# Tiles of 16 channels by 8 states in a selective scan: two tiles share one broadcast of du and one GpSimd product

## The chip, the core and the metric

One core of a Trainium2 chip. The metric is the device time of one execution in microseconds. The engines run side by side and wait for one another by semaphores: TensorE (PE, with its weight loads, PEld), VectorE (DVE), ScalarE (ACT), GpSimd (POOL), and SyncE (SP), which here issues nearly all DMAs in its own program order.

## What is computed

Two layers over a batch of 8 images of 64 x 64 pixels and 96 channels, all in float32. Layer 0 is a two-dimensional selective scan block; layer 1 is an MLP between an FFT upsampling and a low-pass with downsampling. Nearly all time goes to the scan of layer 0, which in the reference is

```
h = exp(dl[..., None] * A) * h + (dl * ul)[..., None] * Bl[:, :, None, :]
y = einsum('bkdn,bkn->bkd', h, Cl)
```

for each of 4096 pixels in four directions k, with 192 channels d and 16 states n. So there are 8 x 4 x 192 x 16 recurrences, each 4096 steps long. Directions 0 and 2 walk the image by rows (forward and back), directions 1 and 3 by columns.

## The kernel before

**Tiles.** A scan tile is 128 partitions by T = 1024 pixels: 16 states by 8 channels. A chunk of 1024 pixels of one direction holds 192 / 8 = 24 tiles (NT); a direction has 4 chunks, an image 16, the run 128 chunks or 3072 tiles. Inside a chunk, tile i has q = i // 8, and of i % 8 the lowest bit is s and the rest is j, so tiles i and i + 2 with even j lie side by side in channels.

**The life of a tile t** (line numbers of the profile):

- `fetch` (L1074): SP issues a DMA that spreads 8 rows of du = delta * u from DRAM over 128 partitions, each row 16 times (512 KB), into `dub` (4 buffers). It is issued 6 tiles ahead.
- `product_b` (L1080): GpSimd multiplies `dub` by `br`, the repeated B, into `bb` (4 buffers), 3 tiles ahead.
- `decay` (L1087, L1095): six TensorE matmuls with the 0/1 matrix `sel_b` spread delta over the states into PSUM (`pd`, 2 buffers), and ScalarE takes `exp` of it in place with the rate `neg_a` per partition. It is issued one tile ahead.
- `scan` (L1102): VectorE runs the recurrence over the 1024 pixels.
- `product_c` (L1108): the result times `cr`, the repeated C, on VectorE, or on GpSimd for every third tile (i % 3 == 2, `by_pool`).
- `hold` (L1122): the last column goes to `carry` for the next chunk; by VectorE, or by ScalarE for the tiles with `by_pool`.
- `sums` (L1141): every second tile, TensorE adds two tiles' products over the states with `sel_r` into `py`; `store` copies `py` and writes it to DRAM.

Every engine takes its instructions in program order. The loop at the end of the kernel writes the order out by hand; for tile i it issues

```
fetch(tiles[i + FETCH])            # FETCH = 6
product_c(tiles[i - 1])            # GpSimd's tiles
product_b(tiles[i + LEAD])         # LEAD = 3
decay(tiles[i + 1]); scan(t); product_c(t); hold(t)
side.advance(...)                  # other work, up to a budget
sums(tiles[i - 3 : i - 1])         # odd i
```

**Side work.** Everything else is cut into generators that the class `Side` advances once per tile within budgets per engine (`CAPS`, us per tile, and KB for DMA): normalisation and convolution of the next image (`front`), the preparation of the next chunk (`prepare`: loads of u, projections, delta, `dp`, the product du = delta * u on GpSimd at L1040, and `br` and `cr`), and for the image before the layer norm and gate (`tail`) and the MLP (`mlp`). `prepare` fills `br` and `cr` by DMAs straight from the SBUF tile `xd` (L1005). `front` keeps the image transposed in `xt` and writes it to DRAM by `lay` once all blocks are there, so that the row directions read contiguous rows. `tail` loads the row directions' sum into `ye` as a whole image, and GpSimd adds it block by block (L687). At the end of the run, `tail` and `mlp` of the last image run with no scan beside them.

Of the kernel before, what the change touches and what calls it, by code (L numbers as in the profile page):

```python
# [8 lines left out]
F32 = mybir.dt.float32  # L9
# [29 lines left out]
class Side:  # L39
# [10 lines left out]
    CAPS = dict(pe=(2.5, 3.2), act=(2.3, 3.0), dve=(1.5, 1.5), pool=(1.4, 2.7), dma=(270, 450))  # L50
# [87 lines left out]
def kernel(ctx: ExitStack, tc: tile.TileContext, a: dict, out: bass.AP):  # L138
# [32 lines left out]
    for p in range(2):  # L171
# [21 lines left out]
    neg_a = cp.tile([128, K, NT], F32, name="neg_a")  # L193
    queue().dma_start(
        neg_a.rearrange("p k g -> p (k g)"),
        a["a_logs"].rearrange("(c n) k f q j -> n c (k f q j)", n=NS),
    )

    sel_r = cp.tile([128, 4, 32], F32, name="sel_r")
    queue().dma_start(  # L200
        sel_r.rearrange("p j m -> p (j m)"), a["sel_r"].rearrange("(c n) j m -> n c (j m)", n=NS)
    )

    sel_b = cp.tile([128, 8, NS, 8], BF16, name="sel_b")
# [68 lines left out]
    def constants_in():  # L273
        nc.gpsimd.memset(xp, 0.0)
        raw["sel"] = tile_([128, 8, 128], "sel_0")
        for hf in range(2):
            nc.sync.dma_start(
                raw["sel"][64 * hf : 64 * hf + 64].rearrange("p j m -> p (j m)"),
                a["sel_b"][0:64, 0:2].rearrange("r q j m -> r (q j m)"),
            )  # L280
        raw["dt_b"] = tile_([C, K, HF], "dt_b")
        nc.sync.dma_start(raw["dt_b"], a["dt_b"])
        names = ("xp_dt", "xp_c", "xp_b")
        raw["xp"] = [tile_([128, K, Q3, R if n == "xp_dt" else NS], n) for n in names]
        ds = raw["ds"] = tile_([128, Q3, K], "ds")
        for hf in range(2):
            for q, r0, r1, f, c0 in pieces:
                rows, src = slice(64 * hf + r0, 64 * hf + r1), slice(c0, c0 + r1 - r0)
                for t, name in zip(raw["xp"], names):
                    nc.sync.dma_start(t[rows, :, q, :], a[name][src, :, f, 0 : t.shape[-1]])  # L290
                nc.sync.dma_start(ds[rows, q, :], a["ds"][src, f, :])
        for name, shape in (("coef", [128, 3, 3]), ("w2", [128, 3, C]), ("b2", [128, C])):
            raw[name] = tile_(shape, name)
            nc.sync.dma_start(raw[name], a[name])

    def constants_of_scans():
        yield {}

        nc.scalar.activation(neg_a, neg_a, AF.Exp)
        nc.vector.tensor_scalar(neg_a, neg_a, -1.0, None, ALU.mult)  # L300
        nc.vector.tensor_copy(sel_b, raw["sel"].rearrange("p j (c n) -> p j n c", n=NS))
# [214 lines left out]
    def front(b):  # L516
# [6 lines left out]
        def begin():  # L523
            yield {}
            pad = v["pad"] = bp.tile([C, W + 2, H + 2], F32, tag="pad", name="pad", bufs=1)
            nc.gpsimd.memset(pad[:, 0, :], 0.0)
            nc.gpsimd.memset(pad[:, W + 1, :], 0.0)
            nc.gpsimd.memset(pad[:, 1 : W + 1, 0:1], 0.0)
            nc.gpsimd.memset(pad[:, 1 : W + 1, H + 1 : H + 2], 0.0)
            v["xt"] = [bp.tile([128, H, w], F32, tag=f"xt{w}", name=f"xt{w}", bufs=1) for w in (W, W // 2)]  # L530
            u_dram[b] = [dr.tile([DI, L], F32, tag=f"u{o}", name=f"u{o}") for o in range(2)]
            z_dram[b] = dr.tile([DI, L], F32, tag="z", name="z")

        def piece(g):
# [3 lines left out]
            t = bp.tile([128, 4, C], F32, tag="x", name="x", bufs=4)  # L538
# [34 lines left out]
        def conv(n, g):  # L573
# [5 lines left out]
            for tap in range(9):  # L579
# [11 lines left out]
            xt = v["xt"][n]  # L591
            nc.scalar.copy(
                xt[:, :, 8 * g : 8 * g + 8].rearrange("p h w -> p w h"), e.rearrange("p (i j) -> p i j", i=8)
            )
            for rows, cs, blk in parts_of(n, g):
# [3 lines left out]
                )  # L599

        def lay(n):

            yield {}
            while not all((b, n, blk) in filtered for blk in range(8)):
                yield {}
            for h0 in range(0, H, 8):
                yield dict(dma=262 if n == 0 else 131)
                h1 = h0 + 8
                if n == 0:
                    src = v["xt"][0][:, h0:h1].rearrange("p h w -> p (h w)")  # L610
                    nc.sync.dma_start(u_dram[b][0][0:128, W * h0 : W * h1], src)
                else:
                    u = u_dram[b][0][128:192].rearrange("c (h w) -> c h w", h=H)
                    for p in range(2):
                        nc.sync.dma_start(u[:, h0:h1, 32 * p : 32 * p + 32], v["xt"][1][64 * p : 64 * p + 64, h0:h1])
            yield {}
            laid.add((b, n))
# [21 lines left out]
        lays = [(4, 0, lambda n=n: lay(n)) for n in range(2)]  # L639
# [4 lines left out]
        if b == 0:  # L644
            return start + convs[:4], convs[4:] + lays + gates + [bp.close(), bp.close()]
        return start, convs + lays + gates + [bp.close()]

    def tail(b, keep, pairs=True):
# [3 lines left out]
        def begin():  # L652
# [4 lines left out]
            v["ye"] = [bp.tile([C, H, W], F32, tag=f"ye{f}", name=f"ye{f}", bufs=1) for f in range(HF)]  # L657
            for h0 in range(0, H, 8):
                for f in range(HF):
                    yield dict(dma=200)  # L660
                    nc.sync.dma_start(
                        v["ye"][f][:, h0 : h0 + 8].rearrange("p h w -> p (h w)"),
                        y_dram[b][0][f * C : f * C + C, W * h0 : W * h0 + 8 * W],
                    )
            yield {}
            yield {}

        def block(g):
# [6 lines left out]
            for t, src in zip(yz, (y_dram[b][1], z_dram[b])):  # L675
                for f in range(HF):
# [3 lines left out]
                    )  # L680
            y, z = [yz[0][:, f] for f in range(HF)], yz[1]
            yield {}
            yield {}
            yield dict(pool=2.6)
            for f in range(HF):
                e = v["ye"][f][:, :, 8 * g : 8 * g + 8].rearrange("p h w -> p w h")
# [96 lines left out]
    def mlp(b, keep):  # L783
# [13 lines left out]
        def up_h(j):  # L797
# [3 lines left out]
            for wh in range(2):  # L801
# [4 lines left out]
                s.append(bp.tile([SIDE, MB], F32, tag="t1s", name="t1s", bufs=5))  # L806
# [9 lines left out]
        def fetch_rows(r0):  # L816
            s = v[r0] = bp.tile([128, 5, C], F32, tag="t1r", name="t1r", bufs=4)
# [14 lines left out]
        def rows_(r5):  # L832
# [12 lines left out]
            xu = bp.tile([C, px], F32, tag="xu", name="xu", bufs=4)  # L845
            nc.scalar.activation(xu, t[:C, :px], AF.Identity, scale=got["rs"], bias=got["nb"])  # L846
            for m in range(3):
                yield dict(pe=0.95, act=0.7)
                if m == 0:
                    sq = bp.tile([128, 3, px], F32, tag="mq", name="mq", bufs=3)  # L850
                t = side.again(n, "ph")
                nc.tensor.matmul(t[:, :px], w1[:, m, :], xu, start=True, stop=True)  # L852
                nc.scalar.activation(sq[:, m, :], t[:, :px], AF.Square, bias=b1[:, m : m + 1])  # L853
            yield dict(pe=0.95)
            t = side.again(n, "p3")
            for j in range(15):
# [3 lines left out]
                    t[:SIDE, C * i : C * i + C], sq[:, m, row], w2q[:, m, :], start=(m == 0), stop=(m == 2)  # L860
# [95 lines left out]
    def prepare(b, k, i0, got):  # L956
# [3 lines left out]
        def begin():  # L960
# [4 lines left out]
            assert k % 2 or all((b, n) in laid for n in range(2))  # L965
# [31 lines left out]
        def broadcasts():  # L997

            xd = v["xd"]
            for name, row in (("br", 48), ("cr", 32)):  # L1000
                t = got[name] = pp.tile([128, T], F32, tag=name, name=name)
                for hf in range(2):
                    yield dict(dma=256)
                    src = xd[64 * hf + row : 64 * hf + row + NS, None, :]
                    nc.sync.dma_start(t[:, MB * hf : MB * hf + MB], src.to_broadcast([NS, 8, MB]))  # L1005
# [47 lines left out]
    for b in range(images):  # L1053
        for k in (1, 0, 2, 3):
            order = range(NCH) if k < 2 else range(NCH - 1, -1, -1)
            for n, c in enumerate(order):
                got = {}
                for i in range(NT):
                    q, n8 = divmod(i, 8)
                    s, j = n8 % 2, n8 // 2  # L1060
                    tiles.append(
                        dict(b=b, k=k, i0=c * T, first=n == 0, i=i, q=q, s=s, j=j, g=8 * q + 4 * s + j, got=got)
                    )
# [6 lines left out]
    def fetch(t):  # L1070
        assert t["got"].get("ready", 0) > t["q"]
        t["dub"] = sp.tile([128, T], F32, tag="dub", name="dub", bufs=4)
        g = t["g"]
        nc.sync.dma_start(  # L1074
            t["dub"], t["got"]["du"][None, 8 * g : 8 * g + 8, :].to_broadcast([NS, 8, T])
        )

    def product_b(t):
        t["bb"] = sp.tile([128, T], F32, tag="bb", name="bb", bufs=4)
        nc.gpsimd.tensor_tensor(t["bb"], t["dub"], t["got"]["br"], ALU.mult)  # L1080

    def decay(t):
        pd = t["pd"] = psd.tile([128, T], F32, tag="pd", name="pd")
        for p in range(3):
            for hf in range(2):
# [3 lines left out]
                    sel_b[rows, 4 * t["s"] + t["j"]].rearrange("p n c -> p (n c)"),  # L1089
# [5 lines left out]
        nc.scalar.activation(pd, pd, AF.Exp, scale=neg_a[:, t["k"], t["g"] : t["g"] + 1])  # L1095

    def scan(t):
# [3 lines left out]
        held = carry[:, t["g"] : t["g"] + 1]  # L1101
# [4 lines left out]
    def product_c(t):  # L1106
        t["hc"] = sp.tile([128, T], F32, tag="hc", name="hc", bufs=4)
        (nc.gpsimd if t["by_pool"] else nc.vector).tensor_tensor(t["hc"], t["h"], t["got"]["cr"], ALU.mult)  # L1108
# [9 lines left out]
    def hold(t):  # L1118
        if t["last"]:
# [3 lines left out]
            carry[:, t["g"] : t["g"] + 1], t["h"][:, end : end + 1]  # L1123
# [8 lines left out]
    def sums(two):  # L1132
# [5 lines left out]
        for t in two:  # L1138
            for hf in range(2):
# [3 lines left out]
                    sel_r[:, t["j"], :],  # L1143
# [40 lines left out]
    LEAD, FETCH = 3, 6  # L1184

    with tc.manual_schedule():
# [8 lines left out]
        side.urgent = prepare(0, tiles[0]["k"], tiles[0]["i0"], tiles[0]["got"])  # L1195
# [4 lines left out]
        for i in range(FETCH):  # L1200
            fetch(tiles[i])
            if i >= FETCH - LEAD:
                product_b(tiles[i - FETCH + LEAD])
# [3 lines left out]
        for i in range(n + 4):  # L1207
# [41 lines left out]
            if i + FETCH < n:  # L1249
                fetch(tiles[i + FETCH])  # L1250
            if 0 < i <= n and tiles[i - 1]["by_pool"]:
                product_c(tiles[i - 1])
            if i + LEAD < n:
                product_b(tiles[i + LEAD])
# [112 lines left out]
```

## Time and profile before

| | |
|---|---|
| time, median of 3 runs | 10879.19 us (10876.58 to 10884.08) |
| the profiled execution | 10889.88 us, its span 10888.1 us |
| granted TensorE clock | 0.977 |
| busy | POOL 93%, DVE 92%, PE 86%, ACT 63% |
| DMA | 2402.30 MB, queue q1 87.0% of 16 engines |
| first product of B on GpSimd, and the last scan | start at 136.8 and 10610.4 us |

A group of instructions is read as: line, engine, operation, tile written <- tiles read, count, then busy time in us and mean ns of one, then the engine's idle time ahead of them with what ended most of it. A line of waits gives the total us, the number of waits and the longest.

### The profile page before, as it was taken

The page shows a single profiled execution, that of the slowest core. Times are in us where ns is not written, and L with a number is a line of the kernel's source. Part 1 is how long each engine was busy: PE and PEld are TensorE (multiplying, and loading weights), DVE is VectorE, ACT ScalarE, POOL GpSimd, SP SyncE. Part 2 cuts the span into 40 slices and gives each one's busy share as a digit, 9 for nine tenths or more (in the row PEclk, how much of TensorE's full clock was granted, in tenths as well). Part 3 has the DMA queues.
Part 4 walks back from the last instruction along what each step waited for, and adds up shares of the span by engine and source line. Part 5 has one row for each costly group of instructions (what it writes and reads, how often), then busy time and mean ns, then how long its engine had stood idle before and what let it go on. Part 6 is the DMA issues. An engine that isn't in the chain of part 4 may idle for free. (4 is left out here: it accounts for less than half of the span.)

```text
span 10888.1 us, 152912 instructions
## 1 busy us (share of the span) xinstructions
PE 9406.6 (86%) x52498; PEld 3129.1 (29%) x52498; DVE 9965.6 (92%) x7319; ACT 6891.4 (63%) x10138; POOL 10172.5 (93%) x4674
## 2 busy tenths in 40 slices
PE   7788778988789988899889997898978989789888
PEld 2222222422233222332223322233222432223325
DVE  5999999999999999999999999999999999999990
ACT  5666556767567665666656666566756767566653
POOL 4999999999999999999999999999999999999990
PEclk8999999999999999999999999999999999999998
DMA  6879898898988989898998989899898898988981
GB/s 155 224 200 234 218 236 216 221 235 232 239 214 225 235 233 233 214 225 232 240 228 220 230 223 247 217 225 234 231 237 218 222 232 234 239 214 223 230 207 49
DMA packets 1052725, 2402.30 MB, mean 221 GB/s; under 512 B 302012, under 2 KB 322748, under 8 KB 1051944
## 3 DMA queue, kind: packets, MB, share of 16 engines
q1 hardware_dynamic: 1050968, 2391.48, 87.0%
q8 instruction: 413, 6.77, 0.3%
q14 instruction: 368, 3.01, 0.1%
q10 hardware_dynamic: 976, 1.04, 0.0%
HBM read 1929.05 MB, written 328.73 MB: 207 GB/s over the span
## 5 line engine op out<-in xcount | busy, mean ns | idle before, releaser
L1080 POOL TENSOR_TENSOR bb<-dub,br 128x1024 f32<-128x1024 f32 x3072 | 7183.5, 2367 | 149.2 <-DMA dub<-du 95.6
L1095 ACT ACTIVATE pd<-pd,neg_a 128x1024 f32<-128x1024 f32 x3072 | 3339.4, 1087 | 3051.3 <-PE pd L1087 3026.1
L1102 DVE TENSOR_TENSOR_SCAN pd<-pd,carry,bb 128x1024 f32<-128x1024 f32 x1536 | 3605.4, 2347 | 279.3 <-ACT pd L1095 162.6
L1087 PE MATMUL pd<-dp,sel_b 64*128 64x512 bf16 x18432 | 2596.7, 385 | 1075.4 <-DVE carry L1122 686.6
L1108 DVE TENSOR_TENSOR hc<-pd,cr 128x1024 f32<-128x1024 f32 x2048 | 2508.7, 1225 | 144.8 <-PE py L1141 3.2
L1108 POOL TENSOR_TENSOR hc<-h,cr 128x1024 f32<-128x1024 f32 x1024 | 2423.0, 2366 | 180.3 <-DVE h L1102 151.4
L1102 DVE TENSOR_TENSOR_SCAN h<-pd,carry,bb 128x1024 f32<-128x1024 f32 x768 | 1797.5, 2341 | 1.7 <-ACT pd L1095 1.6
L1141 PE MATMUL py<-hc,sel_r 128*32 128x512 f32 x12288 | 1736.0, 620 | 48.6 <-POOL hc L1108 47.1
L1087 PEld LDWEIGHTS <-sel_b 64*128 64x128 bf16 x18432 | 722.7, 94 | 3602.7 <-issue 1557.1
L1102 DVE TENSOR_TENSOR_SCAN pd<-pd,bb 128x1024 f32<-128x1024 f32 x512 | 1173.3, 2292 | 128.2 <-ACT carry L1122 52.2
L565 PE MATMUL pc<-pad,convr 96*128 96x512 f32 (+1 forms) x2304 | 844.0, 610 | 2.1 <-issue 2.1
L1115 PE MATMUL idle<-xp,ident 128*128 128x384 f32 x1450 | 662.9, 540 | 3.2 <-ACT t1s L807 3.2
L1102 DVE TENSOR_TENSOR_SCAN h<-pd,bb 128x1024 f32<-128x1024 f32 x256 | 583.7, 2280 | 14.8 <-ACT pd L1095 11.6
L1040 POOL TENSOR_TENSOR u<-dl,u 128x512 f32<-128x512 f32 x384 | 491.7, 1280 | 108.7 <-ACT dl L1035 108.7
L1017 PE MATMUL pv<-xd,dt_w 64*64 64x512 f32 x1536 | 425.4, 632 | 166.9 <-ACT xd L994 164.5
L1141 PEld LDWEIGHTS py<-hc,sel_r 128*32 128x32 f32 x12288 | 253.4, 109 | 977.2 <-issue 751.4
L859 PEld LDWEIGHTS p<-w2q,mq 128*100 128x100 f32 x4800 | 461.9, 168 | 169.3 <-issue 135.2
L852 PE MATMUL ph<-xu,w 96*128 96x500 f32 x960 | 493.6, 617 | 16.0 <-ACT xu L846 9.2
L859 PE MATMUL p<-w2q,mq 128*100 128x96 f32 x4800 | 504.2, 256 | 2.3 <-ACT mq L853 2.3
L1032 PE MATMUL pv<-e,ident 128*128 128x512 f32 x768 | 437.1, 651 | 27.9 <-ACT pv L1030 27.0
L1042 ACT CAST dp<-pv 128x512 bf16<-128x512 f32 x768 | 452.1, 589 | 5.0 <-PE pv L1041 5.0
L984 PE MATMUL px<-u,xp 64*64 64x512 f32 x1536 | 417.2, 618 | 5.1 <-DMA u<-u 3.2
(162 smaller groups left out, 8195.4 us busy)
## 6 DMA issues: line engine op xcount, KB each, us to landing
dub<-du SPq DMA_DIRECT2D x3072, 512.0 KB
u<-u SPq DMA_DIRECT2D x768, 128.0 KB
du<-u SPq DMA_DIRECT2D x768, 128.0 KB
y<-yq SPq DMA_DIRECT2D x768, 128.0 KB
br<-xd SPq DMA_DIRECT2D x256, 256.0 KB
cr<-xd SPq DMA_DIRECT2D x256, 256.0 KB
yp<-y SPq DMA_DIRECT2D x384, 128.0 KB
yp<-u SPq DMA_DIRECT2D x192, 128.0 KB
```

Of the source, the lines that this page charges most:

```text
L565: nc.tensor.matmul(t[rows].rearrange("p (i j) -> p i j", i=8), weights[:, cs], v["pad"][:, 8 * blk + kw : 8 * blk + kw + 8, kh : kh + H], ...
L852: nc.tensor.matmul(t[:, :px], w1[:, m, :], xu, start=True, stop=True)
L859: nc.tensor.matmul(t[:SIDE, C * i : C * i + C], sq[:, m, row], w2q[:, m, :], start=(m == 0), stop=(m == 2))
L1040: nc.gpsimd.tensor_tensor(v["u"][:, q, :], dl, v["u"][:, q, :], ALU.mult)
L1042: nc.scalar.copy(dp[:, p, :], t)
L1080: nc.gpsimd.tensor_tensor(t["bb"], t["dub"], t["got"]["br"], ALU.mult)
L1087: nc.tensor.matmul(pd[:, MB * hf : MB * hf + MB], sel_b[rows, 4 * t["s"] + t["j"]].rearrange("p n c -> p (n c)"), t["got"]["dp", t["q"]][r ...
L1095: nc.scalar.activation(pd, pd, AF.Exp, scale=neg_a[:, t["k"], t["g"] : t["g"] + 1])
L1102: nc.vector.tensor_tensor_scan(t["h"][:, ::step], pd[:, ::step], t["bb"][:, ::step], 0.0 if t["first"] else held, ALU.mult, ALU.add)
L1108: (nc.gpsimd if t["by_pool"] else nc.vector).tensor_tensor(t["hc"], t["h"], t["got"]["cr"], ALU.mult)
L1115: nc.tensor.matmul(p, ident, xp[:, 0:2].rearrange("p k q r -> p (k q r)"), start=True, stop=True)
L1141: nc.tensor.matmul(py[r0 : r0 + 32], sel_r[:, t["j"], :], t["hc"][:, MB * hf : MB * hf + MB], start=(t["j"] == 0), stop=(t["j"] == 3 and t ...
```

## The change

Partitions of a scan tile become 16 channels by 8 states. The tiles i and i + 2 (j even and odd) now hold the same 16 channels with the lower and the upper 8 states (`half`). They share one `dub` (16 rows of du, each 8 times, 512 KB), and one GpSimd instruction over 2 x 1024 elements multiplies it by both halves of `br`. `br` is now 2 x 1024 wide and `cr` has a tile for each half; both are read from a DRAM copy `bc` of the B and C rows, and the second half of `cr` is read at a chunk's last tile. `neg_a`, `sel_b` and `sel_r` are laid out to fit. To make room, the transposed pieces shrink: `xt` holds 16 of the 64 columns and is written out in runs of 16 floats as soon as two blocks are there, `ye` is read in pieces of 16 columns per block pair, and `x`, `t1s`, `t1r`, `xu` and `mq` have fewer buffers. The DMA budget of the side work rises.

```diff
-    CAPS = dict(pe=(2.5, 3.2), act=(2.3, 3.0), dve=(1.5, 1.5), pool=(1.4, 2.7), dma=(270, 450))
+    CAPS = dict(pe=(2.5, 3.2), act=(2.3, 3.0), dve=(1.5, 1.5), pool=(1.4, 2.7), dma=(450, 700))
...
+        def lay(n, two):
+            yield {}
+            xt, u = v[n, two], u_dram[b][0].rearrange("c (h w) -> c h w", h=H)
+            for h0 in range(0, H, 16):
+                yield dict(dma=131)
+                h = slice(h0, h0 + 16)
+                for rows, cs, blk in parts_of(n, 2 * two):
+                    nc.sync.dma_start(u[cs, h, 8 * blk : 8 * blk + 16], xt[rows, h, :])
...
+            if ("ye", g // 2) not in v:
+                ye = v["ye", g // 2] = bp.tile([C, HF, H, 16], F32, tag="ye", name="ye", bufs=2)
+                for f in range(HF):
+                    src = y_dram[b][0][f * C : f * C + C].rearrange("c (h w) -> c h w", h=H)
+                    for h0 in range(0, H, 32):
+                        yield dict(dma=200)
+                        nc.sync.dma_start(
+                            ye[:, f, h0 : h0 + 32, :], src[:, h0 : h0 + 32, 16 * (g // 2) : 16 * (g // 2) + 16]
+                        )
...
-                s.append(bp.tile([SIDE, MB], F32, tag="t1s", name="t1s", bufs=5))
+                s.append(bp.tile([SIDE, MB], F32, tag="t1s", name="t1s", bufs=4))
...
+    def repeat(got, name, half):
+        if name == "cr":
+            t = got[name, half] = pp.tile([128, T], F32, tag=name, name=name, bufs=3)
+        else:
+            if half == 0:
+                got[name] = pp.tile([128, 2, T], F32, tag=name, name=name)
+            t = got[name][:, half, :]
+        r0 = NS * (name == "br") + 8 * half
+        nc.sync.dma_start(t, got["bc"][None, r0 : r0 + 8, :].to_broadcast([NS, 8, T]))
...
-            xd = v["xd"]
-            for name, row in (("br", 48), ("cr", 32)):
-                t = got[name] = pp.tile([128, T], F32, tag=name, name=name)
-                for hf in range(2):
-                    yield dict(dma=256)
-                    src = xd[64 * hf + row : 64 * hf + row + NS, None, :]
-                    nc.sync.dma_start(t[:, MB * hf : MB * hf + MB], src.to_broadcast([NS, 8, MB]))
+            bc = got["bc"] = dr.tile([2 * NS, T], F32, tag="bc", name="bc")
+            yield dict(dma=128)
+            for hf in range(2):
+                nc.sync.dma_start(bc[:, MB * hf : MB * hf + MB], v["xd"][64 * hf + 32 : 64 * hf + 64, :])
+            yield {}
+            yield {}
+            for name, half in (("br", 0), ("br", 1), ("cr", 0), ("cr", 1))[: 4 if first else 3]:
+                yield dict(dma=512)
+                repeat(got, name, half)
...
-    def fetch(t):
-        t["dub"] = sp.tile([128, T], F32, tag="dub", name="dub", bufs=4)
-    def product_b(t):
-        t["bb"] = sp.tile([128, T], F32, tag="bb", name="bb", bufs=4)
-        nc.gpsimd.tensor_tensor(t["bb"], t["dub"], t["got"]["br"], ALU.mult)
+    def fetch(m):
+        t = tiles[m]
+        t["dub"] = sp.tile([128, T], F32, tag="dub", name="dub", bufs=3)
+        r0 = 64 * t["q"] + 32 * t["s"] + 8 * t["j"]
+        nc.sync.dma_start(t["dub"], t["got"]["du"][r0 : r0 + 16, None, :].to_broadcast([16, 8, T]))
+    def products_b(m):
+        t = tiles[m]
+        bb = sp.tile([128, 2, T], F32, tag="bb", name="bb", bufs=3)
+        for half in range(2):
+            tiles[m + 2 * half]["bb"] = bb[:, half, :]
+        nc.gpsimd.tensor_tensor(bb, t["dub"][:, None, :].to_broadcast([128, 2, T]), t["got"]["br"], ALU.mult)
+    def ahead_of(i, first, second):
+        m = i + (first, None, second)[i % 4 - 1] if i % 2 else None
+        return m if m is not None and 0 <= m < len(tiles) else None
...
-            if i + FETCH < n:
-                fetch(tiles[i + FETCH])
+            if (m := ahead_of(i, 7, 6)) is not None:
+                fetch(m)
+            if i % NT == NT - 1 and i + 1 < n:
+                repeat(tiles[i + 1]["got"], "cr", 1)
             if 0 < i <= n and tiles[i - 1]["by_pool"]:
                 product_c(tiles[i - 1])
-            if i + LEAD < n:
-                product_b(tiles[i + LEAD])
+            if (m := ahead_of(i, 3, 2)) is not None:
+                products_b(m)
```

So at i = 4a + 1 the product for tiles 4a + 4 and 4a + 6 is issued, and at i = 4a + 3 that for tiles 4a + 5 and 4a + 7; a `dub` is fetched four tiles before that.

## The prediction

> **What bounds the kernel now.** I read the busy times first, then the costliest groups, then who waits for whom in the stretch from 300 to 10600 us, which leaves out start and end.
>
> ```profile
> PE 9406.6 (86%) x52498; PEld 3129.1 (29%) x52498; DVE 9965.6 (92%) x7319; ACT 6891.4 (63%) x10138; POOL 10172.5 (93%) x4674
> q1 hardware_dynamic: 1050968, 2391.48, 87.0%
> ```
>
> Three resources look full: GpSimd, VectorE, the DMA queue. Busy shares can't tell which is the limit; the waits can.
>
> ```profile
> L1080 POOL TENSOR_TENSOR bb<-dub,br 128x1024 f32<-128x1024 f32 x3072 | 7183.5, 2367 | 149.2 <-DMA dub<-du 95.6
> L1108 POOL TENSOR_TENSOR hc<-h,cr 128x1024 f32<-128x1024 f32 x1024 | 2423.0, 2366 | 180.3 <-DVE h L1102 151.4
> L1040 POOL TENSOR_TENSOR u<-dl,u 128x512 f32<-128x512 f32 x384 | 491.7, 1280 | 108.7 <-ACT dl L1035 108.7
> ```
>
> ```profile
> DVE pd L1102 <- ACT pd L1095: 200.2, 244, 2.8
> DVE pd L1102 <- ACT carry L1122: 110.5, 142, 3.7
> DVE pd L1102 <- POOL bb L1080: 46.3, 30, 4.2
> DVE h L1102 <- ACT pd L1095: 13.2, 16, 2.0
> ```
>
> ```profile
> PE py L1141 <- POOL hc L1108: 43.6, 45, 2.8
> ```
>
> ```profile
> POOL hc L1108 <- DVE h L1102: 138.3, 153, 2.7
> POOL bb L1080 <- DMA dub<-du: 89.5, 85, 3.0
> POOL bb L1080 <- DVE pd L1102: 32.6, 44, 2.4
> ```
>
> ```profile
> SPq L1074 <- POOL bb L1080: 3636.4, 1861, 7.0
> ```
>
> VectorE's waits are for ScalarE's decay (200 + 110 + 13 = 324 us). GpSimd keeps it waiting some 49 us in 3072 tiles. GpSimd in turn waits for VectorE's scans, and SP stands 3.6 ms waiting for GpSimd to free a `dub`. So VectorE sets the pace, GpSimd runs just ahead of it, and DMA and SP run ahead of both. VectorE's own work is left as it is by this change. The timeline gives its pace and GpSimd's:
>
> ```profile
> 5000.41 2.35 DVE L1102 TENSOR_TENSOR_SCAN pd<-pd,carry,bb 128x1024 f32<-128x1024 f32 x1
> 5003.94 2.34 DVE L1102 TENSOR_TENSOR_SCAN h<-pd,carry,bb 128x1024 f32<-128x1024 f32 x1
> 5006.36 2.36 DVE L1102 TENSOR_TENSOR_SCAN pd<-pd,carry,bb 128x1024 f32<-128x1024 f32 x1
> 5007.85 2.35 POOL L1108 TENSOR_TENSOR hc<-h,cr 128x1024 f32<-128x1024 f32 x1
> 5010.16 2.34 POOL L1080 TENSOR_TENSOR bb<-dub,br 128x1024 f32<-128x1024 f32 x1
> 5012.47 1.26 POOL L1040 TENSOR_TENSOR u<-dl,u 128x512 f32<-128x512 f32 x1
> 5013.70 4.67 POOL L1080 TENSOR_TENSOR bb<-dub,br 128x1024 f32<-128x1024 f32 x2
> ```
>
> A plain tile takes VectorE 3.53 us from scan to scan (3.58 over several), a tile whose product by C is GpSimd's 2.42 (2.25 elsewhere; I take 2.35). GpSimd starts its next instruction 2.31 us after a 1024-element product and 1.23 us after `u`.
>
> **The double product.** 2048 elements in one instruction have no row. From above: two of today's, 4.73 us. From below: the step from 512 to 1024 elements is 2367 - 1280 = 1087 ns, so 2367 + 2 x 1087 = 4.54 us; lower I see no reason for. I take 4.54, as the work per element stays. GpSimd saves 1536 x 0.19 = 296 us of work; off the path. What can reach the end is what it now holds up: the 49 us, and the 44 us for which TensorE waits for its product by C and delays decays. I count -49 (the new waits come next) and -20 of the 44, the rest being covered by VectorE's own lead.
>
> **The coarser step.** `bb` had four buffers of one tile; it gets three of two. The product for tiles 4a+5 and 4a+7 takes the buffer of 4a and 4a+2, so it can't begin before scan 4a+2 ends, and scan 4a+5 needs it: three tiles, where the old one had four. Followed through with the rows above, in the changed program's GpSimd order: after scan 2 (a GpSimd tile) come its product by C, 2.31, and the product for 5, 4.54; with two handovers 7.0 us, against tiles 3 and 4, 7.16 us. Covered by 0.15. From scan 5 on, GpSimd has the product for 8 (4.54), `u` (1.23; it stands there in 119 of 128 chunks), product C of 5 (2.31) and the product for 9 (4.54): 12.62 us. VectorE reaches scan 9 after 2 x 2.35 + 2 x 3.58 = 11.86. Short by 0.76 - 0.15 = 0.6 us. Tiles 17 and 21 repeat it with another `u` ahead of the product for 20, so 256 times in the run: 155 us if VectorE never waited for anything else. It does: the 324 us above and 412 us of its side work (rows of `st`, `e`, `ty`) are 0.24 us per tile, 1.4 us over those six tiles on average, but unevenly. I take 4 in 10 of the places late by 0.35 us: 36 us. The layer norm's additions (L687, 128 of 1.53 us, in pairs of 3 us) fall into such a stretch half the time: 32 x 2.2 = 70 us. Together +106; from 0, if VectorE's hold-ups fall right, to 250 with no cover (155 + 32 x 3.0), and 400 if the double product is 4.73 (three of them per stretch: 256 x 0.57 more).
>
> **DMA and SP.** Mean packet times in the trace's records: 13.4 ns for 128 bytes (65,536 of them), 123 ns for 2048, 258 ns for 4096. `dub` loses 1536 x 128 packets of 4096: -3170 us of 16 engines, -29.1% of the span. `br` and `cr` go from 65,536 packets of 2048 to as many of 4096, +5.1%; `bc` +0.6%. The transposed pieces are 2 x 393,216 runs of 64 bytes: at the 128-byte row +6.0%, less 2.0% for what they replace. From 87.0% to about 68%. This hides behind GpSimd's queue already (its 90 us of waiting for `dub` held up 49 us at most), so it is worth nothing beyond the terms above.
>
> The Trainium skill speaks against the small runs: "DMA: Bandwidth & Descriptors", Specifications, puts the smallest transfer at line rate at 512 bytes and has a read-modify-write below it. No row here shows that for 64 bytes; an estimate at twice the trace's 512-byte packet (26.9 ns) would add 18% and leave the queue at some 86%, where it is now.
>
> SP issues 1536 fewer `dub` at 0.54 us and gains 256 `bc` and 64 `u`. New waits on it: `br` and `cr` behind `bc` (two steps are left for it), and the second half of `cr` behind product C of tile 21; behind that stands the fetch at the next odd tile, which waits longer for its own buffer. The half is needed at tile 26, some 9 us after; uncovered it would cost up to 2 us per chunk, 256 us. I put it at nothing.
>
> **Start, end, buffers.** The first scan waits for a product of 4.54 in place of 2.35 us: +2. The `bc` trip lies beside the deltas (`cr` was issued at 97.5, the first product began at 136.8). At the end the last blocks wait for `ye` too: four DMAs of 3072 runs behind `ty` and `tz`, 0.6 us to issue and about 2.6 us (3072 x 13.4 / 16) each: +8, between 3 and 15. ScalarE waits 65 us for `t1s` buffers today; with four for five it gets worse, +8 (0 to 30). The other cut buffers: 0 to 20, taken as nothing, since their readers come earlier on the same in-order engines.
>
> **Sum** against the profiled execution: 10889.9 + 106 - 49 - 20 + 2 + 8 + 8 = 10945. The median of the runs lies 10.7 below that execution: 10934 us, 0.5% slower.
>
> **Rivals.** *GpSimd's relief carries through* (0.25): VectorE's uneven waiting covers the coarse step, the 106 shrinks to 20 or less; then -31, up to -75 if all 93 us go: 10804 to 10850. For it: 296 us less work on an engine that is 97% busy in the steady part. Against: VectorE hardly waits for it. *No change* (0.17): lateness of about 50 us fills in time that VectorE would have spent waiting for decays. *GpSimd falls behind* (0.13), slower by over 1%: the double product near 4.73 or more `u` and additions in the tight stretches; +150 to +400, 11030 to 11280. It decides where the product for 4a+5 ends after scan 4a+4 in most chunks. *The wide operand or the small runs are dear* (0.05): if the repeated operand cost what the strided addition does (1527 against 1280 ns, +19%), 12 tiles would take GpSimd 44 us against today's 40.9, some 11700 us; if a 64-byte run cost a 2048-byte packet, the queue would pass 100%, over 12000 us. My forecast, slower by 0.2 to 1%, has the remaining 0.40.
>
> About 0.2% (22 us) is what a measurement of this kernel can tell from no change: faster 0.25, same 0.17, slower 0.58. The range goes from 10800, the full relief, to 11130, a third of the way into falling behind.
>
> **What the new profile would show.** Right: `bb` x1536 near 4.5 us, POOL some 300 us less busy, DVE as busy as now, queue q1 near 68%, VectorE's waits for `bb` over 90 us and bunched at tiles 5, 9, 17 and 21 of a chunk, waits for decays a little shorter. Wrong: waits for `bb` under 40 us (then faster), a double product over 4.8 us, GpSimd waiting for `dub` or `cr`, or a large change in the waits for decays, which I take to stay.

## The result, and the profile after

The changed kernel takes 10960.92 us (median of 4 runs, 10939.79 to 10967.36) beside 10880.22 us for the kernel before in the same session: a ratio of 1.0071, 95% interval 1.0058 to 1.0083. It is 0.7% slower. The profiled execution took 10967.36 us.

First, where on the span the time lies. I cut each trace at the first and at the last scan (us):

| kernel | start, to the first scan | loop, first to last scan's start | end, after the last scan |
|---|---|---|---|
| before | 139.2 | 10471.2 | 275.3 |
| changed | 143.5 | 10526.5 | 293.2 |
| difference | +4.3 | +55.3 | +17.9 |

Then the page: busy times, the DMA queue and GpSimd's groups.

```profile
PE 9485.0 (86%) x52574; PEld 3149.6 (29%) x52574; DVE 9968.0 (91%) x7319; ACT 6879.4 (63%) x10139; POOL 9954.9 (91%) x3138
q1 hardware_dynamic: 1543800, 1737.14, 64.7%
L1104 POOL TENSOR_TENSOR bb<-dub,br 128x2048 f32<-128x2048 f32 x1536 | 6949.1, 4532 | 28.5 <-DMA dub<-du 13.9
L1141 POOL TENSOR_TENSOR hc<-h,cr 128x1024 f32<-128x1024 f32 x1024 | 2413.0, 2356 | 556.6 <-DVE h L1135 445.4
```

The two loads that the change was to lift are lighter: GpSimd has 218 us less work, and the queue went from 87% to 65%. VectorE's 9968 us are the same as before. So the loss is not in work but in waits: VectorE's idle time inside the loop is 600 us where it was 548, and that is 52 of the 55 us. The granted TensorE clock was lower, 0.970 in this execution for 0.977, but it doesn't go with the times: of the experiments below, e6 is the slowest at 0.983, and e12 and e13, both near 0.97, differ by 25 us. VectorE's waits from 300 to 10600 us (total us, times, longest):

```profile
DVE pd L1135 <- ACT pd L1128: 234.0, 318, 2.4
DVE pd L1135 <- POOL bb L1104: 80.7, 75, 6.3
DVE pd L1135 <- ACT carry L1155: 38.8, 52, 3.0
DVE h L1135 <- POOL bb L1104: 26.2, 22, 7.8
DVE hc L1141 <- PE py L1174: 23.2, 23, 2.2
DVE h L1135 <- ACT pd L1128: 9.3, 8, 2.1
```

The waits for `bb` rose from 49 to 107 us, with a longest of 7.8 us where it was 4.2. Those for ScalarE fell from 324 to 282. Waits of its products by C for TensorE's sums (`hc` behind `py`) rose from 3 to 23 us; e2 below has 17 of these, so most of them don't come from the wide instruction. GpSimd waits for VectorE more than it did, and hardly at all for `dub`:

```profile
POOL hc L1141 <- DVE h L1135: 420.8, 275, 4.8
POOL bb L1104 <- DMA dub<-du: 8.0, 9, 1.9
```

An engine that waits 421 us and still delivers late 97 times is one whose work comes at the wrong moments. The timeline shows one such place, tiles 17 to 21 of a chunk. GpSimd:

```profile
5448.93 1.27 POOL L1062 TENSOR_TENSOR u<-dl,u 128x512 f32<-128x512 f32 x1
5450.16 4.51 POOL L1104 TENSOR_TENSOR bb<-dub,br 128x2048 f32<-128x2048 f32 x1
5454.63 2.99 POOL L696 TENSOR_TENSOR ty<-ty,ye 96x512 f32<-96x512 f32 x2
5457.59 2.34 POOL L1141 TENSOR_TENSOR hc<-h,cr 128x1024 f32<-128x1024 f32 x1
5459.90 4.50 POOL L1104 TENSOR_TENSOR bb<-dub,br 128x2048 f32<-128x2048 f32 x1
```

and VectorE beside it (the scans of tiles 17, 20 and 21):

```profile
5449.00 2.29 DVE L1135 TENSOR_TENSOR_SCAN h<-pd,bb 128x1024 f32<-128x1024 f32 x1 [0.45 <-POOL bb L1104]
...
5458.32 2.28 DVE L1135 TENSOR_TENSOR_SCAN h<-pd,bb 128x1024 f32<-128x1024 f32 x1
5464.44 2.30 DVE L1135 TENSOR_TENSOR_SCAN pd<-pd,bb 128x1024 f32<-128x1024 f32 x1 [3.83 <-POOL bb L1104]
```

Between 5448.93 and 5464.40 GpSimd never rests: `u`, the product for 20 and 22, two additions of the layer norm, tile 17's product by C, and last the product for 21 and 23. VectorE is through with tiles 17 to 20 at 5460.6 and stands 3.8 us. Over the run I counted the gaps of more than 150 ns ahead of scans that ended as the scan's own `bb` was ready, the first scan of the run left out: 109 us, of which 66 lie at tile 21, 23 at 17, 16 at 9 and 3 at 5. Half of them (54 us) lie in the first direction of an image, the one in which most of those additions run.

### The profile page after: what moved, and what is told of

Its sections match the earlier page's. It is cut to its first block, busy times and chain, and to the rows that moved or that the text cites. A ratio compares the mean times of both kernels' runs of the same rounds, so it can differ in the third digit from the quotient of the medians.

```text
span 10965.6 us, 146187 instructions
## 1 busy us (share of the span) xinstructions
PE 9485.0 (86%) x52574; PEld 3149.6 (29%) x52574; DVE 9968.0 (91%) x7319; ACT 6879.4 (63%) x10139; POOL 9954.9 (91%) x3138
## 3 DMA queue, kind: packets, MB, share of 16 engines
q1 hardware_dynamic: 1543800, 1737.14, 64.7%
## 5 line engine op out<-in xcount | busy, mean ns | idle before, releaser
L1104 POOL TENSOR_TENSOR bb<-dub,br 128x2048 f32<-128x2048 f32 x1536 | 6949.1, 4532 | 28.5 <-DMA dub<-du 13.9
L1174 PE MATMUL py<-hc,sel_r 128*32 128x512 f32 x12288 | 1716.6, 623 | 4.7 <-POOL hc L1141 4.7
L1148 PE MATMUL idle<-xp,ident 128*128 128x384 f32 x1526 | 704.2, 544 | 17.7 <-ACT t1s L816 12.1
```

The costliest lines, as they stand in the source:

```text
L1104: nc.gpsimd.tensor_tensor(bb, t["dub"][:, None, :].to_broadcast([128, 2, T]), t["got"]["br"], ALU.mult)
L1148: nc.tensor.matmul(p, ident, xp[:, 0:2].rearrange("p k q r -> p (k q r)"), start=True, stop=True)
L1174: nc.tensor.matmul(py[r0 : r0 + 32], sel_r[:, t["j"] // 2, :], t["hc"][:, MB * hf : MB * hf + MB], start=(t["j"] == 0), stop=(t["j"] == 3 ...
```

## The experiments

Three theories. **A**: the double product is ready too late, because its buffer is given back late, or because of its place in GpSimd's order. **B**: the small transposed pieces, the fewer buffers and the larger DMA budget cost the time. **C**: the sharing costs by itself; at first I meant the extra reads of `bc`, `cr` and the shared `dub`, from e6 on anything that goes with a 4.5 us instruction. Of all kernels I read the loop beside the total, as start and end move on their own. The loop is that of one profiled execution, and the changed kernel's own runs differ by 28 us, so a loop that differs by 20 us says little alone; where much hangs on a difference I give the medians' beside it:

| kernel | time, us | ratio to before | 95% interval | loop, us | end, us |
|---|---|---|---|---|---|
| e1 product ahead of product C | 10933.24 | 1.0058 | 1.0045 to 1.0071 | 10505.1 | 297.5 |
| e2 single products | 10878.67 | 1.0003 | 0.9994 to 1.0012 | 10439.0 | 291.9 |
| e3 before, with pieces and budget | 11327.1 | 1.0414 | 1.0399 to 1.0428 | 10884.9 | 302.1 |
| e4 ye read early | 10933.24 | 1.0055 | 1.0039 to 1.0070 | 10498.9 | 272.7 |
| e6 adjacent tiles | 11531.86 | 1.0590 | 1.0575 to 1.0604 | 11088.9 | 295.4 |
| e7 = e2 and e4 | 10860.16 | 0.9976 | 0.9966 to 0.9987 | 10436.9 | 273.4 |
| e8 before, budget alone | 11006.35 | 1.0110 | 1.0096 to 1.0124 | 10578.4 | 278.7 |
| e9 before, pieces alone | 11295.01 | 1.0372 | 1.0358 to 1.0386 | 10862.5 | 287.5 |
| e10 adjacent, sums shifted | 10975.38 | 1.0084 | 1.0071 to 1.0098 | 10534.2 | 291.8 |
| e11 = e10, four cr, two dub, e4 | 11111.42 | 1.0205 | 1.0191 to 1.0219 | 10692.1 | 273.5 |
| e12 four pairs, even issue | 10916.73 | 1.0040 | 1.0027 to 1.0052 | 10473.0 | 295.4 |
| e13 four pairs alone | 10941.40 | 1.0064 | 1.0050 to 1.0078 | 10516.5 | 292.9 |

**e1, another order in the step.**

```diff
+            if (m := ahead_of(i, 3, 2)) is not None:
+                products_b(m)
             if 0 < i <= n and tiles[i - 1]["by_pool"]:
                 product_c(tiles[i - 1])
-            if (m := ahead_of(i, 3, 2)) is not None:
-                products_b(m)
```

> The changed kernel with one swap: in each loop step GpSimd's double product by B is issued ahead of its product by C, no longer behind it. Theory A (coarse step: the 55 us lost between first and last scan come from the double product, which can begin only after scan 4a+2 and then stands in order behind a product by C and behind u): product 5 and 17 end 2.3 us earlier, so the waits for bb (109 us over 150 ns each, 104 of them at tiles 9, 17 and 21 of a chunk) fall under 40 us, the time per tile from 3.428 to 3.405-3.415 us, the median to 10890-10930 us. Theory B (the small transposed pieces, the fewer buffers and the larger DMA budget of the side work cost the loop time): nothing moves, 10950-10970 us. Theory C (the reads of bc, cr and the shared dub hold the loop up): nothing moves, or worse, since GpSimd's product by C comes later.

The loop fell by 21 us, which is within the spread of the runs, the gaps for `bb` only from 109 to 96 us; at tile 21 they stayed (63 us). A swap inside a step moves a product past a product by C of the same step. The product by C ahead of tile 21's product belongs to an even step, in which no double product is issued, so it is not passed. Less than theory A had promised.

**e2, single products.** The change with two single products for each wide one. With the wide instruction go its three pairs of `bb` and its issue three and two tiles ahead in turn; here each product is issued three tiles ahead into one of four single `bb`. e2 also gives `dub` a fourth buffer, which can be worth little: the changed kernel waited 8 us for `dub`.

```diff
-        t["dub"] = sp.tile([128, T], F32, tag="dub", name="dub", bufs=3)
+        t["dub"] = sp.tile([128, T], F32, tag="dub", name="dub", bufs=4)
...
-        bb = sp.tile([128, 2, T], F32, tag="bb", name="bb", bufs=3)
-        for half in range(2):
-            tiles[m + 2 * half]["bb"] = bb[:, half, :]
-        nc.gpsimd.tensor_tensor(bb, t["dub"][:, None, :].to_broadcast([128, 2, T]), t["got"]["br"], ALU.mult)
...
+        t["bb"] = sp.tile([128, T], F32, tag="bb", name="bb", bufs=4)
+        nc.gpsimd.tensor_tensor(t["bb"], tiles[t["at"]]["dub"], t["got"]["br"][:, t["half"], :], ALU.mult)
...
-            if (m := ahead_of(i, 3, 2)) is not None:
-                products_b(m)
+            if i + 3 < n and i + 3 >= 0:
+                product_b(tiles[i + 3])
```

> The changed kernel with the wide instruction alone undone: the 16 x 8 tiles and the shared dub stay, but each tile gets its product by B from its own GpSimd instruction of 1024 elements, 3 tiles ahead, with four bb of one tile and four dub. Theory A: GpSimd has some 200 us more work, yet waits for bb fall under 50 us and the loop goes back to 3.405-3.415 us per tile; 10890-10915 us, the rest being start and end. Theory B: 10945-10970 us. Theory C: 10945-10970 us, too, since dub, br and cr come as in the changed kernel.

The loop is 87 us shorter than the changed kernel's, and 32 shorter than before's. VectorE's waits, same window, and GpSimd's for `dub`:

```profile
DVE pd L1134 <- ACT pd L1127: 169.2, 243, 2.4
...
DVE pd L1134 <- POOL bb L1103: 34.1, 28, 3.2
```

```profile
POOL bb L1103 <- DMA dub<-du: 9.1, 9, 1.8
```

So the wide instruction, with its buffers and its places in the order, costs 87 us, although it is less work; and the rest of the change is worth 32 us in the loop, most of which start and end take back. By the medians the two are smaller, some 74 us (ratios 1.0071 and 1.0003) and, with start and end taken off, some 18; the profiled execution of the kernel before was a long one. That B is the loss in the loop falls with this run: whatever the pieces cost there, the rest saves more.

**e3, e8, e9: the pieces and the budget on the kernel before.** e3 puts the small pieces, the fewer buffers and the new budget into the kernel before; e8 the budget alone; e9 the pieces and buffers alone.

```diff
-    CAPS = dict(pe=(2.5, 3.2), act=(2.3, 3.0), dve=(1.5, 1.5), pool=(1.4, 2.7), dma=(270, 450))
+    CAPS = dict(pe=(2.5, 3.2), act=(2.3, 3.0), dve=(1.5, 1.5), pool=(1.4, 2.7), dma=(450, 700))
```

> The kernel before with the rest of the change alone: small xt and ye pieces, fewer buffers of x, t1s, t1r, xu and mq, the DMA budget of 450/700; tiles, dub, br, cr and the single products are those of before. Theory A: the loop stays at 3.405-3.42 us per tile, the end (last scan to the end of the span) grows from 275 to 288-296 us; 10885-10910 us. Theory B: the loop goes to 3.42-3.43 us per tile, 10930-10965 us. Theory C: as A.

> The kernel before with nothing but the change's larger DMA budget of side work per tile (450 and 700 for 270 and 450). If the budget is what made e3 dear (bursts of transfers ahead of dub on a queue at 87%), most of e3's 4.1% appears here: 11,150 to 11,330. If the small pieces did it, the time stays within 40 us of 10,880.

> e3 (the kernel before with the change's small transposed pieces and smaller buffers) but with the old DMA budget of 270 and 450. If the small pieces are dear by themselves on a queue at 87%, 11,200 to 11,400, near e3's 11,327. If it was the budget, 10,880 to 10,950. Both in part: between.

e3 was the largest surprise: +4.1%. The pieces and buffers alone make +3.7%, as e9's first case said; the budget alone +1.1%, between e8's two cases. GpSimd's waits for `dub` (89.5 us before), first in e8:

```profile
POOL bb L1080 <- DMA dub<-du: 179.9, 154, 5.9
```

and in e9, with its queue:

```profile
q1 hardware_dynamic: 1752408, 2391.48, 89.4%
POOL bb L1081 <- DMA dub<-du: 480.9, 278, 5.6
```

The queue's share hardly moves (87.0 to 89.4%), but GpSimd's waits for `dub` go up five times, in a window that leaves out the last 400 us of e9's longer loop. By direction, over the images from the second on, the first direction, in which most pieces of `ye` are read, takes 3893 ns per tile for 3557, and the last, in which most pieces of `xt` are written, 3679 for 3447; the two between are as before. In e8 the loss reaches VectorE by another way than `bb`, for which it waits 46 us (before: 49): TensorE waits 107 us for GpSimd's products by C (before: 44), and VectorE's waits for sums and carries grow by 34 and 56 us.

In e2, with the same pieces and budget, a queue at 66% and `dub` shared, the waits for `dub` are 9 us. So with the 16 x 8 tiles the pieces do no harm that shows in the loop. Two things have changed there for `dub`: the queue is emptier, and each buffer serves two tiles and is fetched four tiles ahead of its first product, for three before. No run parts them, but e11 shows that the share isn't all: with two `dub` buffers and a queue at 64.4% GpSimd waits 107 us. How much of e9 is the runs of 64 bytes and how much the fewer buffers was not taken apart either.

**e4 and e7, the end.** The `ye` pieces of the last image are read as soon as their blocks have been added, not behind each block's own loads.

```diff
+            if not pairs and g % 2:
+                while g // 2 < NCH - 2 and v.get(("added", g // 2 + 2), 0) < 2:
+                    yield {}
+                yield from pieces_of(g // 2)
...
+            v["added", g // 2] = v.get(("added", g // 2), 0) + 1
```

> The changed kernel with one edit: for the last image the pieces of ye are read before the block waits for its chunk, so that the last ones are in SBUF when the last scan ends. If the 18 us by which the end grew (275 to 293 us) are the wait for ye: the end falls to 278-284 us, the median to 10945-10952 us, the loop unchanged. If they are the fewer buffers of t1s, t1r, xu and mq: the end stays at 290 us or more.

> Single products (e2) together with the early ye pieces of the last image (e4). If the two are independent, e2's 10,879 less the 18 to 20 us that e4 took from the end: 10,857 to 10,863, 0.2% faster than the kernel before; loop 10,439, end some 272. If the pieces read ahead get in the way of single products, 10,870 or more.

GpSimd's waits after 10620 us, in the changed kernel:

```profile
POOL ty L696 <- DMA ye<-y: 22.9, 3, 19.4
```

and in e4:

```profile
POOL ty L703 <- DMA ty<-y: 8.8, 1, 8.8
```

The end went from 293.2 to 272.7 us, under the 275.3 of before: its whole growth was this wait (before: 9 us there, for `ty`). (e4's loop is 28 us shorter too, as much as the runs of the changed kernel differ; I draw nothing from that.) e7 joins it to single products and comes to 10860.16 us, ratio 0.9976: faster than both kernels, and 18.5 us below e2, about what the end gave.

**e6, tiles of one product side by side.** Now the 87 us. In e6 tiles 2a and 2a+1 share a product, so a pair always comes free four tiles ahead. The second half of `cr`, which is now wanted at a chunk's second tile, is read one step earlier.

```diff
-                    s, j = n8 % 2, n8 // 2
+                    s, j = n8 // 2 % 2, n8 // 4 * 2 + n8 % 2
...
-            tiles[m + 2 * half]["bb"] = bb[:, half, :]
+            tiles[m + half]["bb"] = bb[:, half, :]
...
-            if (m := ahead_of(i, 3, 2)) is not None:
+            if (m := ahead_of(i, 4, 4)) is not None:
...
+            if i % NT == NT - 2 and i + 2 < n:
+                repeat(tiles[i + 2]["got"], "cr", 1)
```

> The changed kernel with the tiles in another order, so that the two tiles of one double product stand next to each other (0 and 1, 2 and 3, ...) and no longer two apart. Double instruction, three pairs of bb, shared dub and small pieces stay. A pair is then given back after its second tile's scan with four tiles in front of the product that wants the buffer, each time; in the changed kernel it was four and two in turn. If the loss is a matter of when a pair comes free (theory A, in its form after e1: the release, not the order in the step), DVE's waits for bb fall from 109 us to some 15 to 30 as in e2, the loop from 10,526 to 10,440 to 10,460 us and the time to 10,875 to 10,900. If the double instruction costs in another way (its reads and writes beside VectorE's, or 4.5 us that can't be broken by a product C: theory C), the waits stay near 100 us and the time within 20 us of 10,961.

VectorE's waits for `bb` fell to 0.3 us, and yet the kernel lost 5.9%. The waits, and TensorE's group in the changed kernel and in e6, say why:

```profile
DVE pd L1135 <- ACT pd L1128: 619.0, 694, 3.3
...
DVE hc L1141 <- DMA cr<-bc: 71.3, 13, 10.0
...
DVE pd L1135 <- POOL bb L1104: 0.3, 1, 0.3
```

```profile
L1174 PE MATMUL py<-hc,sel_r 128*32 128x512 f32 x12288 | 1716.6, 623 | 4.7 <-POOL hc L1141 4.7
```

```profile
L1174 PE MATMUL py<-hc,sel_r 128*32 128x512 f32 x12288 | 2976.4, 605 | 10.2 <-POOL hc L1141 9.8
```

The same 12288 matmuls occupied TensorE for 1716.6 us in the changed kernel (mean 623 ns each, so by the trace, in which the ends of matmuls are modelled, some 4.5 of them overlap). There the four matmuls of a sum write four different groups of 32 rows; in e6 they write two. TensorE rises to 92% of a longer span and its decays come late; e10 tests this. My experiment had changed a second thing.

**e10 and e11, the sums mended.** e10 sums tiles 1 and 2, 3 and 4, 5 and 6 of eight, and 0 and 7 alone; e11 also gives `cr` a fourth buffer and takes one from `dub`.

```diff
-            ends = i % 2 == 1 and 3 <= i <= n + 2
+            two = {1: tiles[i - 2 : i - 1], 3: tiles[i - 3 : i - 2]}.get(i % 8, tiles[i - 3 : i - 1] if i % 2 == 0 and i % 8 != 2 else [])
+            ends = two if 3 <= i <= n + 1 else []
```

> e6 once more, with TensorE's sums mended: tiles of one double product next to each other, as in e6, but the sums are taken for tiles 1 and 2, 3 and 4, 5 and 6 of each eight (which lie in different rows of py, so that their matmuls run side by side again) and for tiles 0 and 7 alone. In e6 no two tiles of a sum could run side by side: py took 2976 us of TensorE for 1717. With three pairs and two singles for four pairs, py should take a quarter more, 2030 to 2150 us, and TensorE some 89% of the span. If e6 lost its time to TensorE alone (theory A), the waits for the decays fall from 664 us to 230 to 300, those for bb stay under 20 us, the waits for the late cr half stay (71 us), and the time is 10,890 to 10,980. If e6 lost it in another way that goes with the adjacent order (theory C), the time stays over 11,300.

> e10 with the late cr half mended too: four buffers for cr, all four halves loaded with the next chunk's other broadcasts, paid for with two buffers of dub for three (du is then fetched right after the product that frees the buffer, four tiles ahead of its use); and the early ye pieces of e4. If the double instruction itself costs nothing once its buffers come free early and nothing else is late (theory A), the loop comes to e2's, 10,440 to 10,490 us, the end to 273, and the time to 10,860 to 10,915, beside e7's 10,860. If two dub buffers are too few, GpSimd waits for dub by over 100 us and the time is 10,950 to 11,100.

TensorE's group in e10:

```profile
L1174 PE MATMUL py<-hc,sel_r 128*32 128x512 f32 x12288 | 2093.3, 617 | 35.4 <-POOL hc L1141 35.4
```

`py` took 2093.3 us, and 555 us of e6's loop came back: e6's loss was TensorE's. No gap for `bb` over 150 ns is left, but the loop is no shorter than the changed kernel's. VectorE's waits in e10:

```profile
DVE pd L1135 <- ACT pd L1128: 254.2, 292, 6.0
DVE pd L1135 <- ACT carry L1155: 72.4, 114, 7.9
DVE hc L1141 <- DMA cr<-bc: 42.6, 7, 9.3
DVE h L1135 <- ACT pd L1128: 14.4, 26, 1.6
```

What was saved on `bb` is paid to the late half of `cr`, to carries and to decays. e11 came out as the second of its two cases: with two buffers GpSimd waits 107 us for `dub`, and the loop grows by 158. The adjacent order cured the symptom and was no test of the cost.

**e12 and e13, a fourth pair in the change's own order.** The cleanest test, with shared constants to make room: e12 and e13 return other values, and only their times are read.

```diff
-        bb = sp.tile([128, 2, T], F32, tag="bb", name="bb", bufs=3)
+        bb = sp.tile([128, 2, T], F32, tag="bb", name="bb", bufs=4)
...
# e12 only:
-        m = i + (first, None, second)[i % 4 - 1] if i % 2 else None
+        m = i + (first, None, second)[i % 4] if i % 2 == 0 else None
...
-            if (m := ahead_of(i, 7, 6)) is not None:
+            if (m := ahead_of(i, 8, 7)) is not None:
...
-            if (m := ahead_of(i, 3, 2)) is not None:
+            if (m := ahead_of(i, 4, 3)) is not None:
```

> The changed kernel's own order of tiles and sums, with a fourth pair of bb and its products issued evenly: one every second tile, four and three tiles ahead in turn (du another four ahead of that), where the changed kernel issued them three and two ahead, at steps two apart. To make room, constants are shared, which changes values and no instruction of the loop: one convolution tap stands for all nine and for the gate's weights, and one block of w1 for three. No buffer of the side work is changed; the setup loads and multiplies a little less, so the loop (first to last scan) is what is read. Theory A (the pair's late release and the uneven issue are the loss): DVE's waits for bb fall from 109 us to under 30 and the loop from 10,526 to 10,440 to 10,465 us. Theory C (a 4.5 us instruction on GpSimd costs by itself, through what stands behind it: product C, u, or the carries): waits for bb fall, but others rise, and the loop stays over 10,500, as in e10.

> e12's fourth pair of bb and its shared constants (one tap for nine and for the gate, one block of w1), but products and fetches issued exactly where the changed kernel has them (three and two ahead; du seven and six). If the release of the pair is the loss, e13's loop comes near e12's. If the place of the issue in GpSimd's order is (a product two tiles ahead, behind a product C and u, is late whatever the buffer), the waits for bb stay at 80 to 109 us and the loop at 10,505 to 10,530, since the product is issued no earlier than two tiles ahead. I expect the second, for a product issued behind the scan before last has its buffer already; a loop between says both.

VectorE's waits for `bb` in e13:

```profile
DVE pd L1136 <- POOL bb L1105: 77.2, 73, 6.5
...
DVE h L1136 <- POOL bb L1105: 27.7, 24, 7.5
```

and in e12 (with the wait for `cr`, new there):

```profile
DVE pd L1136 <- POOL bb L1105: 31.7, 17, 4.0
DVE hc L1142 <- DMA cr<-bc: 25.5, 13, 3.3
```

The buffer alone changes nothing to be seen (gaps 111 us for 109; loop 10 us shorter; ratio 1.0064 for 1.0071, the intervals overlap). With the buffer and products issued four and three tiles ahead in turn, the gaps fall to 32 us and the loop by 53, or by 43 against e13. The medians have less: e12 is 25 us below e13 and, by the ratios, some 34 below the changed kernel; e13's profiled execution was its longest, and all of e12's runs lie below all of e13's. So of the wide instruction's 87 us (74 by the medians), 25 to 53 are its place in GpSimd's order: two tiles ahead is too late for an instruction of 4.5 us that stands behind a product by C and whatever side work falls there. By the program's order the earlier issue has no free buffer without the fourth pair; e12 needs both. e12's loop stays just over theory A's range, its waits for `bb` too.

What remains is 34 us to e2's loop. It doesn't lie ahead of the scans. VectorE's gaps inside the loop, from the traces:

| us | changed | e2 | e12 |
|---|---|---|---|
| over 150 ns, ahead of scans | 405 | 342 | 325 |
| over 150 ns, ahead of products by C | 29 | 22 | 67 |
| shorter ones | 166 | 152 | 167 |

With the wide instruction issued early the scans wait no longer than with single products. Of e12's 67 us, 26 lie at a chunk's fourth tile, behind the late half of `cr`, and 36 at its first. So e12's own order makes `cr` late (e13, with the changed kernel's order, waits 0.6 us for it); why the first product by C of a chunk waits, and why all kernels with the wide instruction have at least 13 us more of the short gaps than e2, no run shows.

## Why the prediction was right

The forecast was 10934 us, the result 10961, inside the range and on the side that had most of the chance. The mechanism that was to cost time, products of B that come late because they come in pairs, is the one that did; that the total came so near is in part luck, as two terms were wrong in opposite directions. By its own terms:

- **Double product, 4.54 us.** Measured mean 4532 ns, start to start 4.48. GpSimd's saving was put at 296 us from busy times; its busy time fell by 218, as a pair of single products takes 4.62 us from start to start. Off the path either way. The rival of the wide operand is out: a repeated operand has no price here.
- **Coarse step +106, old waits -49: net +57.** The waits for `bb` rose by 58 us, and e2 prices the wide instruction at +87 in the loop. The mechanism was named too narrowly: I wrote that the product "can't begin before scan 4a+2 ends". e13 shows that freeing the buffer alone does nothing; the point of issue binds as early. The places were 5, 9, 17 and 21 as forecast. The working had 9 and 21 late and 5 and 17 just covered: 82 of 109 us lie at 9 and 21, but 66 of them at 21 alone, where `u`, the additions and two double products meet. The direction with most of the additions has 54 us (forecast for the additions: 70), the other three 55 (forecast for all places without them: 36).
- **TensorE's waits for product C, -20.** They fell from 43.6 to 4.4 us, as far as they could; what that was worth at the end no run shows:

```profile
PE py L1174 <- POOL hc L1141: 4.4, 5, 2.1
```

- **DMA relief "worth nothing beyond the terms above".** The term that failed most in kind. In e2 the loop is 32 us shorter than before's (some 18 by the medians) with GpSimd's work as it was: waits for `dub` fell from 89.5 to 9.1 us, for decays from 213 to 180. And e9 shows the other side: on the kernel before, the change's own small pieces and fewer buffers cost 3.7%. I had looked at the share of time that the queue was busy, not at how late a transfer lands when others stand ahead of it. The loop was put at +45 us (106 - 49 - 20 + 8) and came to +55, but as +87 for the wide instruction and -32 for the rest: two errors that offset each other.
- **Queue at 68%.** It is 64.7%; the packets of 64 bytes took a mean of 12.7 ns by the trace's records (789,504 of them), below the 13.4 of the 128-byte row. The Trainium skill ("DMA: Bandwidth & Descriptors", Specifications) has a read-modify-write below 512 bytes; the estimate made from it, twice 26.9 ns each and a queue of some 86%, isn't borne out by these records. Whether a read-modify-write takes place they don't show.
- **Start +2, end +8.** +4.3 and +17.9. The end's mechanism was right (e4) and its size wrong: the pieces were priced one after another at 2.6 us, but the block stood up to 19.4 us for them.
- **`t1s` buffers +8.** Wrong sign: ScalarE's waits for the DMA that empties them fell from 65.3 to 21.5 us; another 26.4 us are now for TensorE. It isn't the emptier queue: e9, with the same four buffers and a queue at 89.4%, has 26.4 us in place of the 65.3. The cause stays open:

```profile
ACT t1s L816 <- DMA t<-t1s: 21.5, 7, 3.9
```

- **Late half of `cr`, nothing.** GpSimd waited 11 us for `cr` and VectorE 0.3. The cover is thin: where the order was changed, VectorE waited 71 (e6), 43 (e10) and 25 us (e12) for it.

## What to carry to other kernels

Merging two instructions on an engine that is ahead of the bound saves work that nobody waited for, and makes its deliveries coarser; before doing it, write out what stands in front of the merged instruction at its worst place, side work included, against the time until its first reader. If it is done, issue it earlier and pay for the buffers that this takes; a buffer without the earlier issue, or a swap inside a step, brought little here. And price a DMA change by the transfers that are late, not by the queue's share: near 88%, with `dub` fetched for one tile each, the same pieces and buffers cost 3.7% that at 66%, with shared `dub`, cost nothing to be seen in the loop.

## What the runs showed of the hardware

- With the DMA queue at 87.0% of its engines (before) and at 89.4% (e9), GpSimd waited 89.5 and 481 us for the same 3072 transfers into `dub`. Raising the budget of side transfers per tile alone (e8), with the same bytes and 87.0%, doubled these waits and cost 1.1%.
- Packets of 64 bytes took 12.7 ns each in the changed kernel's records, those of 128 bytes 13.4 ns in the kernel before.
- Four matmuls with 32 output rows each that write four different groups of rows overlap on TensorE (changed kernel: 12288 of them, 623 ns each by modelled ends, in 1717 us: 4.5 at a time); where they write two groups, it is 2.5 at a time (e6: 605 ns each, in 2976 us).
- Two products of 1024 elements take GpSimd 2 x 2.31 us from start to start (before), one of 2048 with a repeated operand takes 4.48 (changed): merging saves 0.14 us per pair.
